# A selective-scan layer followed by linear attention: softplus, the front part and the transfers out moved by a slot, diagonal weights cut into 32x32 blocks

## The chip, the core and the metric

The kernel runs on one core of one Trainium2 chip. The metric is the device time of one launch in microseconds (us). The time before is the median of three runs, 8220.86 us, with runs from 8218.34 to 8221.85 us. PE is TensorE, DVE is VectorE, ACT is ScalarE, POOL is GpSimd, and SP is the engine that issues most of the transfers; "PEq" or "SPq" is the instruction queue of such an engine.

## What is computed

The input x has 4 images, 512 channels and 64 x 64 positions, so 4096 positions in a row. Two residual layers follow each other. Cut to what matters:

```
# layer 0: x = x + L0(group_norm(x))
xn     = layer_norm(tokens)                         # over 512 channels
chunks = 4 groups of 128 channels per image         # 16 sequences of 4096 positions
xi, z  = chunks @ in_proj                           # 256 inner channels each
xc     = silu(causal_conv4(xi))
dt, B, C = split(xc @ x_proj)                       # rank 8, 16 states, 16 states
dt     = softplus(dt @ dt_proj + b)
h[t]   = exp(dt[t] * A) * h[t-1] + dt[t] * xc[t] * B[t]    # 256 channels x 16 states
y[t]   = sum over states of h[t] * C[t]  + xc[t] * D
out    = (y * silu(z)) @ out_proj + skip * chunks
L0     = layer_norm(out) @ proj + b
# layer 1: x = x + L1(group_norm(x))
q, k, v = tokens @ w_qkv + b                        # 8 heads of 64
q, k    = relu(q), relu(k)
kq      = k^T q per head ;  out = (v @ kq) / (sum(kq) + eps) @ w_out + b
```

## The kernel before

The work is cut into 128 steps, `steps = [(b, t, c)]`: image b, tile t of 512 positions (8 per image), channel group c (4). A step has 16 slots (`SLOTS`). For half e of the inner channels (2), for four states at a time (index q, 4), a pair of blocks jj (2) makes one slot g. Partitions hold 32 channels x 4 states, so one slot covers two of the four blocks j of 32 channels.

`slot` (L596) issues, for each slot:

- on POOL, `drive(g + 2)` (L588): the product `bx` of dt*x and B for two blocks; after the second slot of a pair also the copy `st` of the last state and the product of the last 128 columns of `h` with C (L620, L621);
- on DVE, two scans over 512 positions (L610). A scan reads its decay `dA` from PSUM;
- on ACT, after each scan, the decay `dA` of the scan three further on (L584, exp), since there are three `dA` banks;
- on DVE, between the two scans, `product(g - 1)` (L628): `h` times C in the first 384 columns, with C in the PSUM bank `c_all`. After an odd g, it has PE make the next `c_all` (`c_row`, L573; there is one such bank), and then PE adds the states up into `y` (`fold_states`, L639; 4 matmuls side by side).

`AWAY = (2, 10)` names the slots after which DVE may take a long normalization operation. In the slot behind it, `BEHIND = [3, 11]`, the product isn't between the next slot's scans but at the end of the slot itself:

```
if i == 0 and g and (g - 1) % SLOTS not in BEHIND:
    product(g - 1, last)
...
if g % SLOTS in BEHIND:
    product(g, last)
after()
```

Everything else is issued in `after` (L987), at the end of slot s, in program order on each engine's queue: `time_banks` (L486, two PSUM banks `pt`: dt @ dt_proj) in slot 1, `time_steps` (L493, the softplus, between two loads of ACT's function table, L1006 and L1008) in slot 2, `to_rows` (L499, dt and dt*x written to DRAM) and `out_proj` (L661) in slot 3, `with_skip` (L667, the bank `po` read by ACT) in slot 4, and one piece of the `front` (`inputs`, L454: the convolution `pc` in four taps per half, then `pz`) in each of the slots 2, 4, 5, 6, 7 and 8. Slot 10 has `silu` with a table load on each side (L927, L1028), slot 12 and later the pieces of `mixers` (L516). `spread` (L507) loads dt and dt*x back from DRAM, spread over the states, in slot 9 for the next step's first half and in slot 1 for the second.

The other work comes from generators in the queues `ahead`, `late`, `rest` and `light`: the next tile's group and layer norm (`tile_norm`, `normed` L404, `group_norm` L326), the projection after the scan (`projected`, L417), the statistics, and the `attention` of the image before (L682). A piece runs where a credit of matmul work and the count of banks held (`room`, L107, against `limit`) allow. `later(n, what)` (L86) puts an action n slots further on, mostly the eviction of a bank. `po`, `pt`, `pc`, `pz` and all banks of the queues come from one pool of three banks, `ps_w`, taken in turn.

## Time and profile before

| what | value |
|---|---|
| time, median of 3 runs | 8220.86 us (8218.34 to 8221.85) |
| the profiled execution | 8214.62 us |
| its span, first to last instruction | 8212.9 us |
| mean granted TensorE clock | 0.874 |
| DVE busy | 7185.7 us (87%) |
| POOL busy | 6889.7 us (84%) |
| PE busy | 6659.6 us (81%) |
| ACT busy | 5346.7 us (65%) |
| span before the first scan, and after the last | 123 us, 462 us |

The span falls into three parts: 123 us until the first scan, 7627 us of scans, and 462 us after the last scan, in which only the attention of the last image is left. A step takes 59.6 us on average (7627 / 128). The time of the scans' part is the busy time of DVE in it and DVE's idle time; the lines that show this stand in the prediction.

### The profile page before, as it was taken

What the parts mean: (1) busy time and instruction counts of PE and PEld (TensorE: products, weight loads), DVE (VectorE), ACT (ScalarE), POOL (GpSimd) and SP (SyncE); (2) the same over time, 40 slices, a digit from 0 to 9 for tenths busy, and PEclk for the clock granted to TensorE, in tenths of its full rate; (3) what the DMA queues carried; (4) which work ended last, traced back from release to release, by engine and by line L of the source; (5) the groups of instructions that cost most, each with busy time, mean ns of one, the idle gap of its engine ahead of it and who ended that gap; (6) DMA issues with size and microseconds to landing.
All of it is one profiled execution on the core that took longest, in us unless ns stands there. A gap on an engine that the chain in (4) does not pass through costs nothing.

```text
span 8212.9 us, 87683 instructions
## 1 busy us (share of the span) xinstructions
PE 6659.6 (81%) x22496; PEld 2253.4 (27%) x22496; DVE 7185.7 (87%) x6890; ACT 5346.7 (65%) x7841; POOL 6889.7 (84%) x4597
## 2 busy tenths in 40 slices
PE   5677777777888888887788888888788888889699
PEld 1122222112233222332232323332123232333144
DVE  5999999999999999989999999998989999989700
ACT  4666667666676667666677766676766777666421
POOL 4999899999898888889999888888989998888700
PEclk8788878788899989998798999899889998989799
DMA  5666666666666656676666666567666666676412
GB/s 160 161 164 156 151 147 152 155 152 163 158 172 152 156 152 155 171 186 155 168 149 173 162 153 155 151 177 181 153 159 157 156 149 149 153 180 179 116 41 88
DMA packets 829308, 1266.18 MB, mean 154 GB/s; under 512 B 183920, under 2 KB 317568, under 8 KB 816512
## 3 DMA queue, kind: packets, MB, share of 16 engines
q1 hardware_dynamic: 804736, 1222.32, 58.9%
q0 software_dynamic: 16896, 33.56, 2.4%
q10 hardware_dynamic: 7168, 4.71, 0.2%
q8 instruction: 176, 2.88, 0.2%
q14 instruction: 332, 2.72, 0.1%
HBM read 1053.28 MB, written 206.57 MB: 153 GB/s over the span
## 4 chain that ended last, share of the span: by engine, by line
PE 27%; DMA 17%; DVE 17%; POOL 13%; issue 9%; ACT 9%; SPq 8%; POOLq 0%; DVEq 0%; ACTq 0%
DVE h L610 11%; DMA d_all<-d_rows 9%; POOL bx L592 8%; PE pq L120 5%; PE y L120 5%; DVE h L633 5%; SPq L559 5%; PE pc L120 4%; ACT dA L584 4%; DMA b_all<-b_rows 3%; PE pr L120 3%; SPq L513 3%; POOL h L621 2%; PE po L120 2%; PE pp L120 2%
## 5 line engine op out<-in xcount | busy, mean ns | idle before, releaser
L592 POOL TENSOR_TENSOR bx<-d_all,b_all 128x1024 f32<-128x1024 f32 x2048 | 4809.0, 2369 | 92.5 <-DVE h L610 77.1
L610 DVE TENSOR_TENSOR_SCAN h<-dA,st,bx 128x512 f32<-128x512 f32 x3584 | 4436.6, 1271 | 207.2 <-ACT dA L584 191.2
L584 ACT ACTIVATE dA<-d_all,a_t 128x512 f32<-128x512 f32 x4096 | 2765.5, 688 | 1629.8 <-DVE h L610 1579.3
L633 DVE TENSOR_TENSOR h<-h,c_all 128x768 f32<-128x768 f32 x2048 | 1913.9, 935 | 153.2 <-PE c_all L120 142.5
L120 PE MATMUL y<-h,fold 128*32 128x512 f32 x8192 | 1327.3, 725 | 273.2 <-POOL h L621 269.1
L621 POOL TENSOR_TENSOR h<-h,c_sb 128x512 f32<-128x512 f32 x1024 | 1298.4, 1268 | 188.9 <-DMA c_sb<-c_rows 70.6
L120 PE MATMUL c_all<-parts,sel 128*128 128x384 bf16 x1024 | 378.5, 370 | 978.6 <-DVE h L633 977.6
L120 PE MATMUL pc<-xn,w_cv 128*128 128x512 f32 x2048 | 1021.4, 628 | 38.9 <-ACT res L858 12.7
L120 PE MATMUL pq<-w_qk,xa 128*128 128x512 f32 x2048 | 1005.6, 625 | 1.6 <-ACT xa L329 1.6
L610 DVE TENSOR_TENSOR_SCAN h<-dA,bx 128x512 f32<-128x512 f32 x512 | 602.8, 1210 | 76.4 <-ACT dA L584 66.3
L120 PEld LDWEIGHTS <-sel 128*128 128x128 bf16 x1280 | 127.4, 100 | 1710.1 <-DVE h L633 1445.7
L120 PEld LDWEIGHTS pc<-xn,w_cv 128*128 128x128 f32 x2048 | 379.7, 198 | 708.6 <-issue 518.5
L620 POOL COPY st<-h 128x4 f32<-128x4 f32 x1024 | 208.5, 204 | 410.9 <-DVE h L610 383.1
L120 PEld LDWEIGHTS pq<-w_qk,xa 128*128 128x128 f32 x2048 | 404.6, 200 | 476.3 <-issue 449.6
L120 PE MATMUL pr<-xb,m 128*128 128x512 f32 x1024 | 505.0, 633 | 6.2 <-DMA xb<-x 4.2
L120 PE MATMUL pp<-xn,w_pr 128*128 128x512 f32 x1024 | 492.5, 613 | 3.8 <-DVE xn L391 3.8
L120 PE MATMUL pt<-dt,w_dt 32*128 32x512 f32 x512 | 378.2, 943 | 141.2 <-ACT parts L539 126.8
L120 PEld LDWEIGHTS y<-h,fold 128*32 128x32 f32 x8192 | 173.5, 116 | 866.1 <-POOL h L621 446.0
L708 ACT ACTIVATE kq<-pq 128x512 f32<-128x512 f32 x256 | 151.7, 593 | 339.9 <-PE pq L120 338.7
L120 PE MATMUL y<-xz,dg 128*128 128x512 f32 x512 | 364.8, 804 | 0.0
L657 POOL TENSOR_TENSOR xz<-xz 128x512 f32<-128x512 f32 x256 | 325.0, 1270 | 2.7 <-ACT xz L654 2.7
L502 POOL TENSOR_TENSOR dt<-dt,xz 128x1024 f32<-128x1024 f32 x128 | 302.6, 2364 | 25.4 <-DMA c_rows<-dt 20.8
(155 smaller groups left out, 6203.3 us busy)
## 6 DMA issues: line engine op xcount, KB each, us to landing
d_all<-d_rows SPq DMA_DIRECT2D x2048, 256.0 KB, 6.5
b_all<-b_rows SPq DMA_DIRECT2D x4096, 64.0 KB, 2.1
d_rows<-dt SPq DMA_DIRECT2D x256, 512.0 KB, 3.0
c_sb<-c_rows SPq DMA_DIRECT2D x4096, 16.0 KB, 1.8
xs<-in_x_dram SPq DMA_DIRECT2D x32, 1024.0 KB, 7.6
xn<-in_x_dram SPq DMA_DIRECT2D x32, 1024.0 KB, 6.5
xr<-in_x_dram POOLq DMA_DIRECT2D x32, 1024.0 KB, 8.9
x<-xr SPq DMA_DIRECT2D x32, 1024.0 KB, 6.6
```

The lines of the kernel that those rows point to most:

```text
L120: nc.tensor.matmul(out_, lhsT, rhs, **how)
L502: nc.gpsimd.tensor_tensor(f["both"][:, 1], f["both"][:, 0], f["xz"][:, 0], ALU.mult)
L513: nc.sync.dma_start(d[k * BLK : (k + 1) * BLK, v], src)
L559: nc.sync.dma_start(dst[k * BLK : (k + 1) * BLK, :], rows_[q * KS + k, :].partition_broadcast(BLK))
L584: nc.scalar.activation(dAs[k], fs[n]["d_all", e][:, 0, j, :], AF.Exp, scale=a_t[:, e, j, q : q + 1])
L592: nc.gpsimd.tensor_tensor(bxs[g], fs[n]["d_all", e][:, 1, jj * 2 : jj * 2 + 2, :], bc(b_all[g // JJ], 2), ALU.mult)
L610: nc.vector.tensor_tensor_scan(h[:, j, :], dAs.pop(2 * g + i), bxs[g][:, i, :], 0.0 if t == 0 else st[:, c, e, q, j : j + 1], ALU.mult, AL ...
L620: nc.gpsimd.tensor_copy(st[:, c, e, q, :], h[:, :, T - 1])
L621: nc.gpsimd.tensor_tensor(h[:, :, CUT:], h[:, :, CUT:], bc(c_sb.pop(g // JJ), NJ), ALU.mult)
L633: nc.vector.tensor_tensor(own, own, bc(c_all[g // JJ], 2), ALU.mult)
L657: nc.gpsimd.tensor_tensor(f["xz"][:, 1, e, :], f["xz"][:, 1, e, :], f["xz"][:, 0, e, :], ALU.mult)
L708: nc.scalar.activation(qk[i], pq, AF.Relu)
```

## The change

What it does, part by part:

1. The softplus and its two table loads are issued in slot 3 instead of 2, `time_banks` in slot 2 instead of 1, `to_rows` and `out_proj` in slot 4 instead of 3, `with_skip` in slot 6 instead of 4, and the front's pieces in slots 3, 5, 6, 7, 8 and 9. `AWAY` becomes (3, 10), so `BEHIND` becomes [4, 11].
2. `normed` waits two slots between the load of a tile and the first operation on it, `projected` one slot before its accumulating transfer.
3. `to_rows`, `mixers` and `store` issue their transfers to DRAM one slot later than the operation that makes the data; `store` frees its bank before that.
4. The tile `res` has two buffers instead of one.
5. Evictions of attention banks issued in slots 5 to 11 are put two slots later instead of one (`soon`).
6. `limit` is 1 in slots 1 to 5 instead of 15 and 0 to 3, and the pieces marked "two ahead" may start in slot 15 and no longer in 14.
7. The diagonal weights `dg` (D) and `skd` (skip) are kept as 128 x 32 tiles, and each diagonal product is four matmuls of 32 x 32 instead of one of 128 x 128. `ones`, `bqk` and `ident` take less room.

The diff, with a line of context around each edit:

```diff
+    def soon():
+        return 2 if now[0] is not None and 5 <= now[0] % SLOTS < 12 else 1
     def until(*done):
...
     work = {"mm": 0.0}
+    def diagonal(out_, w, rhs):
+        for k in range(P // BLK):
+            r = slice(k * BLK, (k + 1) * BLK)
+            mm(out_[r, :], w[r, :], rhs[r, :], abreast=P // BLK, start=True, stop=False)
...
-    ident = const.tile([P, P], F32, tag="ident", name="ident")
+    ident = wk.tile([P, P], F32, tag="sq", name="ident", bufs=4)
     make_identity(nc, ident)
-    ones = const.tile([P, LANE], F32, tag="ones", name="ones")
+    ones = const.tile([P, 1], F32, tag="ones", name="ones")
     nc.vector.memset(ones, 1.0)
...
     dpar = column(d_par, NH, "dpar")
-    dg = const.tile([P, NH, P], F32, tag="dg", name="dg")
+    dg = const.tile([P, NH, BLK], F32, tag="dg", name="dg")
     for e in range(NH):
-        nc.vector.tensor_scalar(dg[:, e, :], ident, dpar[:, e : e + 1], None, ALU.mult)
+        nc.vector.tensor_scalar(dg[:, e, :], fold, dpar[:, e : e + 1], None, ALU.mult)
     g_sb = column(norm_g, NC, "g_sb")
     b_sb = column(norm_b, NC, "b_sb")
-    skd = ident
+    skd = const.tile([P, BLK], F32, tag="skd", name="skd")
     a_sb = rows(a_log, wk.tile([P, NH, NST], F32, tag="sq", name="a_sb", bufs=4))
...
-    bqk = const.tile([P, 2 * C], BF16, tag="bqk", name="bqk")
-    b_all = wk.tile([P, 2 * C], F32, tag="bx", name="b_all", bufs=3)
-    nc.scalar.dma_start(b_all, b_qkv[0 : 2 * C].partition_broadcast(P))
+    bqk = const.tile([P, C], BF16, tag="bqk", name="bqk")
+    b_qk = wk.tile([P, C], F32, tag="bx", name="b_qk", bufs=3)
+    nc.vector.memset(b_qk, 0.0)
+    for i in range(P // LANE):
+        nc.scalar.dma_start(
+            b_qk[i * LANE : i * LANE + 2, :], b_qkv[0 : 2 * C].rearrange("(j c) -> j c", j=2)
+        )
     bv = column(b_qkv[2 * C : 3 * C], NC, "bv")
...
-    nc.vector.tensor_copy(bqk, b_all)
+    nc.vector.tensor_copy(bqk, b_qk)
     for i in (2, 3):
         r = slice(i * LANE, P)
-        nc.vector.tensor_tensor(b_all[r, :], b_all[r, :], bqk[r, :], ALU.subtract)
-        nc.vector.tensor_copy(bqk[r, :], b_all[r, :])
+        nc.vector.tensor_tensor(b_qk[r, :], b_qk[r, :], bqk[r, :], ALU.subtract)
+        nc.vector.tensor_copy(bqk[r, :], b_qk[r, :])
...
             )
-    nc.vector.tensor_scalar(skd, ident, sk, None, ALU.mult)
+    nc.vector.tensor_scalar(skd, fold, sk, None, ALU.mult)
...
                 mm(
-                    sums[c * LANE : (c + 1) * LANE, :], ones, parts[c],
+                    sums[c * LANE : (c + 1) * LANE, :], ones.to_broadcast([P, LANE]), parts[c],
                     start=True, stop=True, abreast=NC,
...
         nc.sync.dma_start(body, cols(x, b)[:, :, t * T : (t + 1) * T])
+        yield from pause(2)
         yield "free"
...
         yield from until(*taken)
+        yield from pause(1)
...
+        both = f["both"]
         if v:
...
         d_rows = dram.tile([P, NH, T], F32, tag=f"d_rows{v}", name=f"d_rows{v}_{nm}")
-        nc.sync.dma_start(d_rows, f["both"][:, v])
         f["d_rows", v] = d_rows
+        later(1, lambda: nc.sync.dma_start(d_rows, both[:, v]))
...
         b_rows = f["b_rows"] = dram.tile([NST, T], F32, tag="b_rows", name=f"b_rows_{nm}", bufs=3)
-        nc.sync.dma_start(b_rows, dtr[RANK : RANK + NST, :])
         c_rows = f["c_rows"] = dram.tile(
...
         )
-        nc.sync.dma_start(c_rows, dtr[LANE : LANE + NST, CUT:])
+        def rows_out():
+            nc.sync.dma_start(b_rows, dtr[RANK : RANK + NST, :])
+            nc.sync.dma_start(c_rows, dtr[LANE : LANE + NST, CUT:])
+        later(1, rows_out)
         parts = f["parts"] = wk.tile([P, CUT], BF16, tag="parts", name=f"parts_{nm}", bufs=3)
...
     SLOTS = NH * NQ * JJ
-    AWAY = (2, 10)
+    AWAY = (3, 10)
     BEHIND = [s + 1 for s in AWAY]
...
             ys[n, e] = ps_y.tile([P, T], F32, tag="y", name=f"y_{n}_{e}")
-            mm(ys[n, e], dg[:, e, :], fs[n]["xz"][:, 0, e, :], start=True, stop=False)
+            diagonal(ys[n, e], dg[:, e, :], fs[n]["xz"][:, 0, e, :])
         h = hs.pop(g // JJ)
...
         po = f["po"] = work_bank(f"po_{nm}", 0)
-        mm(po, skd, xn[:, c, NTAP - 1 : NTAP - 1 + T], start=True, stop=False)
+        diagonal(po, skd, xn[:, c, NTAP - 1 : NTAP - 1 + T])
         for e in range(NH):
...
                     )
-            return later(1, lambda: add(pk, v == 0))
+            return later(soon(), lambda: add(pk, v == 0))
...
                 pq = work_bank(f"pq_{b}_{i}")
-                mm(
-                    pq, sel[:, 0, 0:1].to_broadcast([P, P]), bqk[:, j * C : (j + 1) * C],
-                    start=True, stop=False,
-                )
+                mm(pq, sel[:, 0, j * BLK : j * BLK + 1].to_broadcast([P, P]), bqk, start=True, stop=False)
                 for c in range(NC):
...
                 qk[i] = both[:, 1 + i % 3, :]
-                ready[i] = later(1, lambda i=i, pq=pq: relu(i, pq))
+                ready[i] = later(soon(), lambda i=i, pq=pq: relu(i, pq))
                 if u:
...
-        kqn = wk.tile([P, NC, P], F32, tag="res", name=f"kqn_{b}", bufs=1)
+        kqn = wk.tile([P, NC, P], F32, tag="res", name=f"kqn_{b}", bufs=2)
         nc.gpsimd.memset(kqn, 0.0)
...
         def store(t, o, pp):
-            res = wk.tile([P, T], F32, tag="res", name=f"res_{b}_{t}_{o}", bufs=1)
+            res = wk.tile([P, T], F32, tag="res", name=f"res_{b}_{t}_{o}", bufs=2)
             nc.scalar.activation(res, pp, AF.Identity, bias=ob[:, o : o + 1])
-            nc.sync.dma_start(cols(out, b)[:, o, t * T : (t + 1) * T], res)
             free()
+            later(1, lambda: nc.sync.dma_start(cols(out, b)[:, o, t * T : (t + 1) * T], res))
...
                         yield "more"
-                later(1, lambda t=t, o=o, pp=pp: store(t, o, pp))
+                later(soon(), lambda t=t, o=o, pp=pp: store(t, o, pp))
                 fetch(t + 1, "b")
...
                             gate(before, 1)
-                        if nxt is not None:
-                            time_banks(nxt, names[n + 1])
                     if s == 2 and nxt is not None:
+                        time_banks(nxt, names[n + 1])
+                    if s == 3 and nxt is not None:
                         nc.scalar.preload_act_table_set("softplus")
...
                         nc.scalar.preload_act_table_set("natural_log_exp_and_others")
-                    if s == 4 and before is not None:
+                    if s == 6 and before is not None:
                         pb_, pt_, pc_ = steps[n - 1]
...
                             add_to(late, leave(pb_, pt_))
-                    if s in (2, 4, 5, 6, 7, 8):
+                    if s in (3, 5, 6, 7, 8, 9):
                         next(front, None)
-                    if s == 3 and nxt is not None:
+                    if s == 4 and nxt is not None:
                         to_rows(nxt, 0, names[n + 1])
                         to_rows(nxt, 1, names[n + 1])
-                    if s == 3 and before is not None:
+                    if s == 4 and before is not None:
                         pb_, pt_, pc_ = steps[n - 1]
...
                         what for k, what in ((0, "wide"), (1, "one ahead"), (2, "two ahead"))
-                        if any(a - 2 * k <= s <= a - k for a in AWAY) or (k == 2 and s >= SLOTS - 2)
+                        if any(a - 2 * k <= s <= a - k for a in AWAY) or (k == 2 and s == SLOTS - 1)
                     ]
...
-                    limit[0] = 1 if s in (SLOTS - 1, 0, 1, 2, 3) else 2
+                    limit[0] = 1 if 0 < s < 6 else 2
                     credit = min(credit + 3.5 - (work["mm"] - seen), 2.6)
```

## Prediction

> **What bounds the kernel now.** I read the page first (part 1, then the costliest groups), then busy time by stretches, DVE's waits in the stretch of the scans, and the timeline where these waits sit.
>
> ```profile
> PE 6659.6 (81%) x22496; PEld 2253.4 (27%) x22496; DVE 7185.7 (87%) x6890; ACT 5346.7 (65%) x7841; POOL 6889.7 (84%) x4597
> ```
>
> The share hides stages, so here is the busy time in the scans up to where attention starts, in the scans after that, and behind the last scan (columns: PE, PEld, DVE, ACT, POOL, clock, DMA share, GB/s):
>
> ```profile
> 123.00:1999.00 1876.00, 1334.47 (x4191) 381.34 (x4191) 1796.09 (x1673) 1279.30 (x1853) 1751.13 (x1168) 0.80 0.64 157
> 1999.00:7750.00 5751.00, 4842.95 (x16680) 1653.58 (x16680) 5322.03 (x5058) 3937.28 (x5795) 5121.44 (x3409) 0.89 0.65 161
> 7750.00:8213.00 463.00, 426.81 (x1508) 195.06 (x1508) 29.26 (x77) 96.92 (x150) 5.08 (x5) 0.95 0.18 59
> ```
>
> DVE is busy 7118 of 7627 us of scans: 93%, POOL 90%. The last 463 us are PE's (92%, at nearly the full clock), the same matmuls before and after. So the change can gain only DVE's idle time in the scans (waits for others, longest first; total, times, longest):
>
> ```profile
> DVE h L610 <- ACT dA L584: 257.5, 146, 49.4
> DVE h L633 <- PE c_all L120: 142.5, 102, 3.7
> DVE kq L715 <- PE pk L120: 78.2, 53, 5.7
> DVE h L610 <- POOL bx L592: 25.1, 25, 2.9
> ```
>
> With small ones it is 544 us. I placed each by counting scans (two a slot, 32 a step):
>
> | DVE waits for | slot | us | waits |
> |---|---|---|---|
> | dA | 3 and 4 | 101 | 44 |
> | dA | 6 | 42 | 31 |
> | dA | 12 | 42 | 42 |
> | c_all | 3 | 30 | 20 |
> | c_all | 7 | 78 | 37 |
> | pk | 5, 6, 10 | 31 | 16 |
> | pk, c_all, dA, bx | 13 to 15 | 102 | 89 |
> | pob, pm, gr | 3 to 5 | 36 | 25 |
> | first decay 49, the rest | | 82 | |
>
> The two costliest, looked at. ACT in a step with c = 0 (idle in brackets):
>
> ```profile
> 1280.34 1.52 ACT L329 ACTIVATE xn<-xn,off_a,gr_a 128x512 f32<-128x512 f32 x2 [2.20 <-DMA xn<-in_x_dram]
> ...
> 1283.06 1.28 ACT L1006 ACT_TABLE_LOAD   x1
> 1284.36 1.26 ACT L495 ACTIVATE dt<-pt,dtb 128x512 f32<-128x512 f32 x2
> 1285.64 1.28 ACT L1008 ACT_TABLE_LOAD   x1
> 1286.94 1.52 ACT L329 ACTIVATE xn<-xn,off_a,gr_a 128x512 f32<-128x512 f32 x2
> ```
>
> and DVE in the same microseconds:
>
> ```profile
> 1289.07 2.46 DVE L610 TENSOR_TENSOR_SCAN h<-dA,st,bx 128x512 f32<-128x512 f32 x2 [3.13 <-ACT dA L584]
> ```
>
> The group norm first waits for its load, then its second half follows the softplus, and the decays come behind both. Of the 44 waits, 39 (98 us) are in the steps with c = 0; softplus alone never made DVE wait, and with one more eviction ahead of it, 0.65 us. Slot 7, on PE and on DVE:
>
> ```profile
> 1181.09 1.88 PE L120 MATMUL pc<-xn,w_cv 128*128 128x512 f32 x4
> 1182.81 1.88 PE L120 MATMUL pp<-xn,w_pr 128*128 128x512 f32 x4
> 1184.52 0.33 PE L120 MATMUL c_all<-parts,sel 128*128 128x384 bf16 x1
> ```
>
> ```profile
> 1184.89 0.95 DVE L633 TENSOR_TENSOR h<-h,c_all 128x768 f32<-128x768 f32 x1 [3.32 <-PE c_all L120]
> ```
>
> c_all stands in PE's queue behind the front and the projection. Starts 1.72 us apart for two full matmuls make a unit of 0.86 us.
>
> **The change, part by part.** DVE's own work stays, so the sum is over its waits. A scan holds DVE 1.19 us and a product 0.85 (distances of their starts). T is the end of slot 3's second scan.
>
> *Group norm behind its load, softplus in slot 3.* Moving with it: two table loads of 1.28, two softplus, and `to_rows` with its POOL product (2.36) and two transfers. The pause takes out the wait for the load (80.5 us of ACT). But in the instruction order of the changed kernel, half of the group norm is still issued behind the softplus, in slot 3, the other half in slot 4. Softplus and loads take 3.88 us; the decay behind them is ready at T + 5.3 and DVE wants it at T + 5.27 plus its extra work there: no slack, as before. With half a group norm (1.43) ahead, DVE waits 1.4 us if it has no statistics (1.2) or long operation (2.18) there. Counted over the steps, 11 are late: **101 becomes 14 us** (0 to 40). The load leaves in slot 0 and is used in slot 3, 10 us later, against 6.5 to land; with that cover gone it costs the old 2.7 us per tile. The two transfers of `to_rows` (512 KB each) now stand in SP's queue behind the b_all and c_sb loads of slots 4 and 5 instead of ahead of them.
>
> *`with_skip` in slot 6, `out_proj` in 4.* ACT waited 105 us for `po`; with a slot more, **42 becomes 10** (0 to 30).
>
> *PE's load.* I counted units between one c_all and the next in both orders (mean over steps, a group of four side by side as one):
>
> | c_all of slot | 0 | 2 | 4 | 6 | 8 | 10 | 12 | 14 |
> |---|---|---|---|---|---|---|---|---|
> | before | 3.5 | 4.9 | 10.6 | 6.0 | 5.0 | 3.6 | 7.4 | 3.7 |
> | after | 3.5 | 6.9 | 7.9 | 6.2 | 5.7 | 3.5 | 7.1 | 3.9 |
>
> The peak of 10.6 (14 in one step of ten) is what slot 7 waits for. At 7.9 units, 6.8 us plus 0.35 for c_all, against 7.65 us of DVE work from slot 4's product to slot 7's, only heavy steps (9 to 10 units) are late: 37 by 0.65 us, 24 in all; at 0.95 a unit (clock 0.9) 50 by 1.3, 64 in all. **78 becomes 35** (15 to 80). Slot 3: **30 becomes 25** (15 to 35).
>
> *A new wait in slot 4.* With `AWAY` 3, slot 4 holds product(3) between its scans and product(4) at its end. Product(3) frees the c_all bank, so product(4) needs a c_all made within one scan; before, slots 2 and 3 shared one, and the next had 3.6 us. Behind this wait on DVE are slot 5's scans, and through them dA, bx and all else. In PE's queue ahead of that c_all stand `pt`, half of `pc` and attention's matmuls. The three banks go round: after two for `pt`, the second further bank taken must wait until the softplus in slot 3 has read the first `pt`, T + 2.8. The trace of before has this wait in small (PE for L495, 44 us with the weight loads). In the changed order, 84 of 127 steps take two or more. With 1, 2 or 4 units behind it, c_all is ready at T + 4.0, 4.9 or 6.6; DVE wants it at T + 3.23 plus its extra work. Steps with a long operation in slot 3 are covered (2.18). Step by step, 37 are late, by 1 to 3.4 us: **0 becomes 89** (30 to 150; the wait overlaps those for dA, of which I counted only the excess).
>
> *Slot 12.* The table loads around silu make DVE wait where it has nothing extra in slot 10: 17 such steps 0.85 us each, and 19 with an eviction `xr` ahead (0.67 us) 1.20 each. The last `pz` copy (0.58) now moves in front of silu in every step, while `soon` takes the `xr` away: 39 x 1.2, **42 becomes 50** (40 to 90; upper end: ACT also waits for `pz`).
>
> *Two-slot evictions, the limit.* pk in 5, 6, 10: **31 becomes 10** (5 to 30). Slots 13 to 15: 12's load falls from 7.4 to 7.1: **102 becomes 90** (50 to 110). Small ones at 3 to 5 and the rest: **118 becomes 100** (85 to 130).
>
> *Transfers later, two `res` buffers.* SP waited 245 us (b_rows), 169 (`res`) and 60 (d_rows) at the head of its queue, holding up the b_all and c_sb loads behind: POOL waited 71 us for c_sb, 55 for `xr` outside the end. DVE waited only 25 us for POOL, so I give this nothing beyond the terms above. Cover: d_rows now leaves 4 slots (13 us) before `spread` reads it, and lands in 3.0 us, 6.6 at most; `b_rows` has a dozen slots. In the end stretch ACT waits 61 us for output transfers, but PE's wait for ACT there is at most the row's 12.7: 0 to 13, taken as 0. Before the first scan: ±5, taken as 0.
>
> *Diagonals.* 384 diagonal products, 256 in `y` and 128 in `po`. `pt` pairs on rows 0 and 32 of the array took 2.08 us for both at half clock where one full product took 1.92: row groups run side by side, but into two banks. `y<-h,fold` has four column groups in one bank, 8 instructions in 1.07 us. Neither is four row groups in one bank. The Trainium skill (page PSUM — Partial Sum Buffer, section "PSUM bank collisions raise a hardware error") quotes that column tiles may share a bank at once, but "different row tiles are not able to access the same PSUM bank at the same time". By the rows the diagonal costs one pass as now, plus a change of array shape: the first instruction of `pt` took 0.69 against 0.59, 0.1 x 384 = 38 us of PE, mostly in slack. By the rule, one after the other, it costs three passes more, 2.6 us. I take the rows, since each block has its own columns and partitions too; the rule is the rival below. No gain on PE either way.
>
> Sum after: 14 + 10 + 25 + 35 + 89 + 50 + 10 + 90 + 100 = 423, from 544: 121 less. The profiled execution, 8214.6, becomes 8094; the median lies 6 above it, so **8100 us** (-1.5%). POOL needs 53.7 us a step (6873 / 128) and the step would take 58.6, so it doesn't take over.
>
> **Rivals.**
> 1. *The wait in slot 4 doesn't come* (c_all early enough as PE's idle shows, or hidden in other waits). For: PE waits 978 us for DVE at c_all rows, so it is often ahead. Against: the bank of `pt`. Then 14 for 89, and slot 7 at 15: 8100 - 95 = 8005.
> 2. *Slot 4 takes it all back*: 150, and 80 in slot 7, since waits on PE meet the half clock (0.80 to 0.89 granted). 8100 + 61 + 45 = 8206, no difference.
> 3. *Slower: diagonals run one after the other.* PE gets 2.6 us more ahead of c_all in slots 4 and 6. In slot 6's stretch 6.8 + 0.35 + 2.6 = 9.7 against 7.65: 2.1 x 126 = 265; in slot 4's some 1.2 x 64 = 80. 8100 + 345 = 8445. It decides from about 1.4 us more per diagonal (0.5 slack, and 121 / 128 to eat the gain). For: the rule. Against: the rows of `pt` and `fold`.
> 4. *The order isn't as meant*: group norm is still behind softplus; that is in the sum.
>
> **How the numbers follow.** Forecast 0.60 (own range 8040 to 8160), rival 1 0.20, rival 2 0.13, rival 3 0.07. The bounds added up one way would reach 7950 and 8310; cut to 8 in 10, 7990 to 8200. What a measurement can tell from no change is 0.2%, 16 us. Faster by more: 0.60 + 0.20 + 0.05 of rival 2; slower: 0.07 + 0.01 of it; 0.07 within.
>
> **What would show it.** Right: DVE waits for dA in slots 3, 4 and 6 together below 50 us; for c_all in slot 7 below half; new waits of L655 for c_all at the end of slot 4, in steps with c = 0 or 3, 2 us each; PE waiting for the softplus row some 40 times or more; ACT's waits for xn's load and for `res` transfers near zero in the scans. Wrong: `y<-xz,dg` rows lasting over 3 us for eight instructions; c_all waits at slot 4 in steps with a long operation; POOL bx waits over 60 us.

## The result, and the profile after

The changed kernel takes 8101.42 us (median of 4 runs, 8097.51 to 8103.36), beside 8219.6 us of the kernel before (8215.61 to 8221.85, 4 runs): ratio 0.9856, 95% interval 0.9839 to 0.9873, 118 us less. The forecast was 8100. The sum under it holds less well than the total, so the profile first. The profiled run took 8103.21 us with a span of 8101.5.

Part 1 of the page, after:

```profile
PE 6487.2 (80%) x24800; PEld 2116.5 (26%) x24800; DVE 7158.1 (88%) x6891; ACT 5365.5 (66%) x7841; POOL 6888.6 (85%) x4597
```

The same three stretches by busy time (PE, PEld, DVE, ACT, POOL, granted clock, DMA share, GB/s); the scans now end at 7631 us:

```profile
119.00:1999.00 1880.00, 1317.96 (x4851) 352.17 (x4851) 1824.07 (x1702) 1307.62 (x1889) 1782.42 (x1190) 0.80 0.66 159
1999.00:7631.00 5632.00, 4682.76 (x18329) 1542.67 (x18328) 5268.42 (x5029) 3927.24 (x5759) 5093.09 (x3390) 0.91 0.66 164
7631.00:8101.00 470.00, 435.23 (x1508) 199.17 (x1508) 28.59 (x76) 97.06 (x150) 4.90 (x5) 0.92 0.18 58
```

The time came out of the scans: 7627.4 us before, 7512.0 after. DVE's waits fell from 544 to 453 us (353 waits to 273; 49 and 46 us of them are the wait of the very first scan, which lies ahead of this part), its busy time (overlap taken off) from 7119 to 7093. The start is 4 us shorter; the end stretch is 8 us longer, at a mean clock of 0.92 instead of 0.95. That is not the change: e5 below leaves that part as it was before, and has 470.9 us at a clock of 0.92 too.

DVE's longest waits in the scans after (total, times, longest; most of the pk row, left out, is the end stretch):

```profile
DVE h L655 <- PE c_all L124: 293.5, 172, 5.7
...
DVE h L632 <- ACT dA L606: 105.4, 54, 46.2
...
DVE h L632 <- POOL bx L614: 12.1, 12, 3.4
```

dA fell by 152 us and c_all rose by 151. Placed by counting scans, as for the forecast (`pk` is attention's bank for k^T q):

| DVE waits for | before | forecast | after |
|---|---|---|---|
| dA, slots 3 and 4 (slot 5 after) | 101 | 14 | 8 |
| dA, slot 6 | 42 | 10 | 0 |
| c_all, slot 3 | 30 | 25 | 0 |
| c_all, end of slot 4 (new) | 0 | 89 | 204 |
| c_all, slot 7 | 78 | 35 | 54 |
| dA, slot 12 | 42 | 50 | 48 |
| pk in 4 to 6 and 10 | 31 | 10 | 6 |
| slots 13 to 15 | 102 | 90 | 46 |
| small ones, first decay, rest | 118 | 100 | 87 |
| sum | 544 | 423 | 453 |

What went, on ACT in a step with c = 0: the group norm no longer waits for its load. It stands behind the softplus with two decays between its halves.

```profile
1265.84 1.26 ACT L512 ACTIVATE dt<-pt,dtb 128x512 f32<-128x512 f32 x2
1267.12 1.28 ACT L1027 ACT_TABLE_LOAD   x1
1268.42 1.52 ACT L344 ACTIVATE xn<-xn,off_a,gr_a 128x512 f32<-128x512 f32 x2
1269.85 1.28 ACT L606 ACTIVATE dA<-d_all,a_t 128x512 f32<-128x512 f32 x2
1271.07 1.50 ACT L344 ACTIVATE xn<-xn,off_a,gr_a 128x512 f32<-128x512 f32 x2
```

What came, at the end of slot 4 of the same step, is product(4) behind a late c_all; the wait is the bracket:

```profile
1269.55 0.95 DVE L655 TENSOR_TENSOR h<-h,c_all 128x768 f32<-128x768 f32 x1 [2.38 <-PE c_all L124]
```

This is the step of the forecast (c = 0 or 3, two units ahead, 2 us each). Over all steps the wait has 67.0 us with c = 0, 50.4 with c = 1, 44.2 with c = 2 and 42.2 with c = 3. The steps with c = 1 and 2 were forecast as covered, because DVE has its long operation in slot 3 there. Here is one, PE and then DVE:

```profile
2233.51 3.78 PE L124 MATMUL pc<-xn,w_cv 128*128 128x512 f32 x4 [2.92 <-DVE xn L406]
2237.23 1.70 PE L124 MATMUL mu_sums_b<-xn,ones 128*32 128x512 f32 x8
2238.86 0.34 PE L124 MATMUL c_all<-parts,sel 128*128 128x384 bf16 x1
```

```profile
2231.20 2.26 DVE L406 TENSOR_TENSOR xn<-xn,var_a 128x2048 f32<-128x2048 f32 x1
...
2239.23 0.95 DVE L655 TENSOR_TENSOR h<-h,c_all 128x768 f32<-128x768 f32 x1 [2.54 <-PE c_all L124]
```

The long operation (L406, the layer norm's multiply by its factor) reads that factor, `var`, from a bank of the pool of three. The softplus banks hold the other two, so `pc` starts only when L406 ends. The long operation delays DVE and, through the bank, PE, so it hides little: the wait is 1.5 us on average over the steps with c = 1 and 2, and 1.7 over those with c = 0 and 3. PE's waits for that row and for the softplus:

```profile
PE pc L124 <- DVE xn L406: 127.2, 61, 3.2
PE pc L124 <- ACT dt L512: 47.0, 27, 2.9
```

### The profile page after: what moved, and what is told of

Its sections match the earlier page's. It is cut to its first block, busy times and chain, and to the rows that moved or that the text cites. A ratio compares the mean times of both kernels' runs of the same rounds, so it can differ in the third digit from the quotient of the medians.

```text
span 8101.5 us, 92105 instructions
## 1 busy us (share of the span) xinstructions
PE 6487.2 (80%) x24800; PEld 2116.5 (26%) x24800; DVE 7158.1 (88%) x6891; ACT 5365.5 (66%) x7841; POOL 6888.6 (85%) x4597
## 4 chain that ended last, share of the span: by engine, by line
DVE 21%; PE 19%; DMA 19%; POOL 15%; issue 10%; SPq 9%; ACT 6%; POOLq 0%; DVEq 0%; ACTq 0%
DVE h L632 13%; POOL bx L614 11%; DMA d_all<-d_rows 11%; DVE h L655 6%; SPq L581 6%; PE pq L124 5%; DMA b_all<-b_rows 4%; SPq L531 3%; ACT dA L606 3%; PE pc L124 3%; PE pr L124 3%; PE y L124 2%; DMA c_sb<-c_rows 2%; POOL h L643 2%; POOL dt L520 1%
## 5 line engine op out<-in xcount | busy, mean ns | idle before, releaser
L632 DVE TENSOR_TENSOR_SCAN h<-dA,st,bx 128x512 f32<-128x512 f32 x3584 | 4425.2, 1268 | 59.0 <-ACT dA L606 49.5
L655 DVE TENSOR_TENSOR h<-h,c_all 128x768 f32<-128x768 f32 x2048 | 1908.8, 932 | 301.9 <-PE c_all L124 293.5
L124 PE MATMUL y<-h,fold 128*32 128x512 f32 x8192 | 1287.8, 705 | 140.7 <-POOL h L643 136.9
L124 PE MATMUL pc<-xn,w_cv 128*128 128x512 f32 x2048 | 1068.2, 657 | 189.4 <-DVE xn L406 127.2
L632 DVE TENSOR_TENSOR_SCAN h<-dA,bx 128x512 f32<-128x512 f32 x512 | 601.6, 1207 | 60.3 <-ACT dA L606 55.9
L124 PE MATMUL y<-xz,dg 32*32 32x512 f32 x2048 | 340.5, 741 | 0.0
L124 PE MATMUL pd<-xz,w_xp 128*128 128x512 f32 x512 | 317.3, 752 | 7.8 <-ACT xz L946 7.8
```

What stands on the lines that cost most here:

```text
L124: nc.tensor.matmul(out_, lhsT, rhs, **how)
L632: nc.vector.tensor_tensor_scan(h[:, j, :], dAs.pop(2 * g + i), bxs[g][:, i, :], 0.0 if t == 0 else st[:, c, e, q, j : j + 1], ALU.mult, AL ...
L655: nc.vector.tensor_tensor(own, own, bc(c_all[g // JJ], 2), ALU.mult)
```

## The experiments

In each, the run of the kernel before on the same chip was 8219 to 8223 us (median). "Waits" are DVE's waits in the scans, by slot as in the table. The figures behind a time are its ratio to the kernel before and the 95% interval of that; the intervals reach some 0.0015 to each side, 12 us, so smaller differences between two runs aren't told apart.

**The diagonals (e4).** The kernel before with the 32x32 blocks alone:

```
-            mm(ys[n, e], dg[:, e, :], fs[n]["xz"][:, 0, e, :], start=True, stop=False)
+            diagonal(ys[n, e], dg[:, e, :], fs[n]["xz"][:, 0, e, :])
-        mm(po, skd, xn[:, c, NTAP - 1 : NTAP - 1 + T], start=True, stop=False)
+        diagonal(po, skd, xn[:, c, NTAP - 1 : NTAP - 1 + T])
```

> The kernel before with one edit alone: the diagonal products of D and of skip as four matmuls of 32x32. Theory A (the four blocks run side by side in one bank): y<-xz,dg busy about 1.4 us per product as now, PE busy within 50 us of 6660, time 8220 within 16 us. Rival D (four row groups of one bank go one after the other): PE busy higher by 384 x 2.6 = 1000 us, time about 8500 us or more.

Measured: 8224.06 us (8217.13 to 8233.55), ratio 1.0009 (1.0 to 1.0018); waits 543 us. The `y` rows of before, of e4, and of the changed kernel:

```profile
L120 PE MATMUL y<-xz,dg 128*128 128x512 f32 x512 | 364.8, 804 | 0.0
```

```profile
L120 PE MATMUL y<-xz,dg 32*32 32x512 f32 x2048 | 370.4, 802 | 0.0
```

```profile
L124 PE MATMUL y<-xz,dg 32*32 32x512 f32 x2048 | 340.5, 741 | 0.0
```

Per diagonal product (256 of them) that is 1.43, 1.45 and 1.33 us. One after the other would have been three passes more, 2.6 us. So the four blocks run side by side, in one PSUM bank. Rival 3 is out, and for this form, in which each block of rows has its own columns and partitions, the measurement decides against the sentence that the prediction quoted from the Trainium skill (page PSUM — Partial Sum Buffer, section "PSUM bank collisions raise a hardware error"). That the blocks would then run one after the other was the prediction's own reading of that sentence, which speaks only of access at the same time. No part of the 118 us comes from here.

**The placement of product(4) (e1, e2).** e1 puts the product back behind slot 3's scans, e2 (`BEHIND = [11]`) puts neither product at the end of its slot:

```
-    BEHIND = [s + 1 for s in AWAY]
+    BEHIND = [3, 11]
```

> The changed kernel with BEHIND = [3, 11] instead of [4, 11]; AWAY stays (3, 10). Product(3) is then at the end of slot 3, so the next c_all is issued to PE ahead of slot 3's front and attention matmuls, and product(4) follows between slot 5's scans. Theory A (the 204 us of waits for c_all at the end of slot 4 come from where the product stands: one scan after the c_all bank came free, and behind slot 3's matmuls in PE's queue): that wait falls below 20 us, slot 7's rises from 54 to about 100 because its stretch on PE gets slot 3's matmuls back, time about 7950 us. Rival B (PE's load and the bank held by softplus set the pace, the place only decides where DVE waits): the 204 us turn up in slots 5 to 7 and the time stays within 20 us of 8101.

> The changed kernel with BEHIND = [11]: product(4) between slot 5's scans, c_all issued where it was. It gets one scan (1.19 us) more. Theory A: each of the 95 waits gets shorter by 1.19 us, 204 us become about 101, slot 7 up by some 15, time about 8010 us. Rival B: the time stays within 20 us of 8101, as the waits move on to slot 7.

Measured: e1 8178.03 us (0.9949, 0.9934 to 0.9964), e2 8086.24 us (0.9836, 0.9821 to 0.9851). In e2 the wait falls from 204 to 116 as theory A has it, but slot 7 rises from 54 to 105 and little is gained: 15 us by the medians, with overlapping intervals. In e1 the wait is gone, but slot 7 has 164 us, slot 9 has 43, dA in slots 5 and 6 has 72 and pk 41: 77 us slower, which neither theory forecast.

**PE's order (e7).** The first half of `pc` moves behind the c_all that product(4) needs:

```
-                    if s in (3, 5, 6, 7, 8, 9):
+                    if s in (4, 5, 6, 7, 8, 9):
                         next(front, None)
```

> The changed kernel with one number changed: the first half of the first convolution (pc) is issued in slot 4 instead of slot 3, so it stands behind the c_all that product(4) needs in TensorE's queue, not ahead of it. Theory A: the wait of product(4) (204 us) is the wait of pc for a bank that the long operation or the softplus still holds: it falls below 60 us in all four kinds of steps; slot 7, with pc's two units more ahead of its c_all, rises from 54 to about 100: 8101 - 95 = about 8005. Theory B: TensorE's load and bank waits in slots 3 to 7 together set the pace: slot 7 takes nearly all (from 54 to 170 or more), and the time is within 20 of 8101.

Measured: 8157.37 us (0.9918, 0.9904 to 0.9932). The wait of product(4) falls from 204 to 45, slot 7 rises from 54 to 203. The row over all places is the same as the changed kernel's 293.5:

```profile
DVE h L655 <- PE c_all L124: 293.1, 169, 5.3
```

Theory B in its mechanism, though the time is 56 us worse, not equal: dA and busy time rose by 27 and 16 us. Moving matmuls about the c_all of slot 4 moves the wait and does not remove it.

**No banks for the queues in slots 2 to 5 (e8).** On top of e2:

```
-                    limit[0] = 1 if 0 < s < 6 else 2
+                    limit[0] = 0 if 1 < s < 6 else 2
```

> The changed kernel with product(4) between the scans of slot 5 (as in e2, 8086 us) and no bank for attention, projection or normalization taken in slots 2 to 5 (limit 0 there instead of 1). Theory A: their matmuls ahead of the c_all of slots 4 and 6 are what is late in slots 5 and 7 (221 us in e2), and later slots have room for them: these waits fall below 80 us and slots 8 to 15 rise by 40 at most: about 8000. Theory B: the work of these queues is needed on time and the slots 6 to 15 are full: the waits move there (slots 8 to 15 rise by 130 us or more), or attention spills behind the last scan and lengthens the end stretch of 470 us: 8090 to 8200.

Measured: 8184.22 us (0.9949, 0.9937 to 0.9962). c_all in slot 5 73 us, slot 7 none, slot 9 136; dA 50 in slot 5 and 69 in slot 12; statistics of `xr` wait 30. The end stretch stays at 470 us. Theory B's shift, with slot 9 as the place.

**The bank that the long operation frees (e9, e10).** The factor goes to SBUF, the order of the instructions is unchanged; e10 adds `BEHIND = [11]`:

```
-            nc.scalar.activation(var, rs, AF.Exp, scale=-0.5)
+            nc.scalar.activation(rs, rs, AF.Exp, scale=-0.5)
-        nc.vector.tensor_tensor(v, v, bc(var, NC), ALU.mult)
+        nc.vector.tensor_tensor(v, v, bc(rs, NC), ALU.mult)
```

> The changed kernel with the result of the exponential (the factor of the layer norm) written to SBUF instead of back into its PSUM bank; the long operation multiplies from there, so the bank that the next convolution (pc) takes comes free one to two slots earlier. The order of the instructions is the same. Theory A (the bank that the long operation frees is what makes product(4) late in the steps with c = 1 and 2): TensorE's waits for L406 (127 us) fall below 15, the waits of product(4) in steps with c = 1 and 2 from 95 to under 35 us, all of them from 204 to about 140, and slot 7 stays near 54: 8101 - 60 = about 8040. Theory B (the load of slots 2 to 7 sets the pace, as e7 showed for another edit): slot 7 takes most of it (54 to 110 or more): within 20 us of 8101. If the long operation costs more from SBUF than the 2.26 us it has now, by 0.3 us or more, that is 128 x 0.3 = 38 us against both.

> e9 together with e2 (product(4) between the scans of slot 5; 8086 us alone). Theory A: the two causes add: 116 + 105 us of waits in slots 5 and 7 fall to about 140 together: 8000 to 8020. Theory B: within 20 us of 8086.

Measured: e9 8107.96 us (0.986, 0.9846 to 0.9873), e10 8075.37 us (0.9822, 0.9808 to 0.9835). In e9's list of PE's longest waits, L406 no longer stands (it was third, with 127 us):

```profile
PE c_all L124 <- DVE h L655: 1193.2, 530, 11.3
PE y L124 <- POOL h L643: 176.1, 200, 3.6
PE pc L124 <- ACT dt L512: 50.0, 26, 2.9
```

The wait of product(4) is 3.8 us in steps with c = 1 and nothing with c = 2 (95 before this edit), still 113 with c = 0 and 3. All of it is 117 (204), and slot 7 stays at 57. The time did not follow, because the long operation got slower, by far more than the 0.3 us that the expectation allowed for (which also multiplied by 128; there are 64). The row of the changed kernel, then that of e9:

```profile
L406 DVE TENSOR_TENSOR xn<-xn,var_a 128x2048 f32<-128x2048 f32 x32 | 72.3, 2260 | 8.3 <-ACT var_a L400 8.3
```

```profile
L406 DVE TENSOR_TENSOR xn<-xn,rs_a 128x2048 f32<-128x2048 f32 x32 | 103.8, 3243 | 6.5 <-ACT rs_a L400 6.5
```

One us more in 64 operations is 64 us, and DVE's busy time is up by 64, while all waits fell by 63.

The slower operation also covers part of the wait, since product(4) itself comes later. In the steps with c = 1 and 2, counted from the end of slot 3's second scan, DVE is ready for product(4) at 5.4 us on average in the changed kernel and at 6.4 in e9; c_all is ready at 6.8 and at 5.8. That c_all comes 1.0 us earlier although everything on DVE is 1.0 us later shows the bank to be the cause. With DVE's times of the changed kernel and c_all's of e9, step by step, 26 of the 95 us would be left; that is an estimate from the two traces, and no run has the early bank without the slow operation.

Why is it slower? In e9's timeline, before the scans, where POOL has no work beside it, the operation takes 2.29 us; beside POOL's `bx` products it takes 3.27:

```profile
69.17 2.29 DVE L406 TENSOR_TENSOR xn<-xn,rs_a 128x2048 f32<-128x2048 f32 x1 [6.54 <-ACT rs_a L400]
```

```profile
2235.33 3.27 DVE L406 TENSOR_TENSOR xn<-xn,rs_a 128x2048 f32<-128x2048 f32 x1
```

```profile
2231.76 4.69 POOL L614 TENSOR_TENSOR bx<-d_all,b_all 128x1024 f32<-128x1024 f32 x2
2236.38 2.26 POOL L642 COPY st<-h 128x4 f32<-128x4 f32 x1
```

POOL's product ends 1.1 us after DVE's operation starts; then POOL's copy of 512 numbers (0.20 us on average in the changed kernel) lasts until the operation ends. All 62 of these operations within the scans show it: each lasts what POOL's product has left when it starts (0.56 to 2.01 us) plus 2.15 us, to 0.01 us. The 58 of POOL's copies that overlap them last 2.25 us on average, the other 966 last 0.20. So one holds up the other in turn, whole instructions at a time. That such a pair contends, for an exclusive lock, is what the Trainium skill (page SBUF — State Buffer, section "Who interferes with whom") states for a VectorE instruction with two SBUF inputs beside a GpSimd instruction that reads SBUF.

e10, where the c_all waits of slots 5 and 7 are 72 and 73 (116 and 105 in e2), is 11 us faster than e2 by the medians (the two intervals overlap) and 26 us faster than the changed kernel, with an interval just below that one's. Theory A's sum (8000 to 8020) did not come: the two waits fell to 145 us as it has it, but the slower operation took most of that back.

**The group norm's pause alone (e5).** The kernel before, with the group norm two slots behind its load:

```
         nc.sync.dma_start(body, cols(x, b)[:, :, t * T : (t + 1) * T])
+        yield from pause(2)
         yield "free"
...
-            assert c != 2 or not ahead
+            assert c != 3 or not ahead
```

The second edit lets the next tile's pieces reach into the step with c = 2; e3, the pause without it, gave no result.

> The kernel before with one edit: the group norm of the next tile is issued two slots behind its load (the softplus stays in slot 2, nothing else moves). Theory A: the waits for dA in slots 3 and 4 of the steps with c = 0 (98 us of before) come from the group norm standing in ACT's queue with its load still under way, and DVE gets them back wherever they stood: 98 to under 20, time 8219 - 80 = about 8140. Theory B: TensorE's load ahead of c_all in slots 5 to 7 sets the pace of these slots, so the wait turns up again as one for c_all in slot 7 (78 us in before becomes 130 or more): 8190 to 8220.

Measured: 8209.68 us (0.9983, 0.9977 to 0.999), waits 538. The waits for dA in slots 3 to 5 fell from 103 to 24 us, in the steps with c = 0 from 98 to 10, as theory A has it. The gain did not come, though not by way of slot 7's c_all, which fell to 53. Now the layer norm's mean is late for the long operation on it (48 of these 54 us are in the scans), the waits for bx rose from 25 to 50, and those for c_all in slots 3 and 15 from 56 to 96:

```profile
DVE xn L371 <- PE mu_a L120: 54.4, 19, 6.4
```

Alone, the pause is worth 13 us. In the changed kernel no wait for `mu_a` is among the scans' waits; which of the other moves takes it away was not tried.

**The transfers and the buffers (e6, e11, e12).** e6 is the changed kernel with all moves in the slots undone. It keeps the transfers out one slot later, the two output buffers and the diagonals (and the smaller constants and the slot's pause ahead of `projected`'s accumulating load, which its expectation did not name):

```
-        yield from pause(2)
-    AWAY = (3, 10)
+    AWAY = (2, 10)
-                    if s == 3 and nxt is not None:
+                    if s == 2 and nxt is not None:
                         nc.scalar.preload_act_table_set("softplus")
...
```

> The changed kernel with all of its moves in the slots undone (front, softplus, products for the rows, out_proj, with_skip, AWAY, limit, two-slot evictions and the pause back as before); what stays are the transfers out one slot later, the two output buffers and the 32x32 diagonals. Theory A (the forecast): these give nothing beyond the moves: 8205 to 8225, DVE waits in the scans as before (544 us) within 25. Theory B: DVE's busy time, 26 us less in the changed kernel, and part of its waits come from transfers that no longer block SP's queue: 8150 to 8190, with DVE busy near 7093 us in the scans.

e11 undoes the late transfers in the changed kernel, e12 the second buffer (`kqn`, which shares it, follows):

```
-        later(1, lambda: nc.sync.dma_start(d_rows, both[:, v]))
+        nc.sync.dma_start(d_rows, both[:, v])
-        later(1, rows_out)
+        rows_out()
...
-            later(1, lambda: nc.sync.dma_start(cols(out, b)[:, o, t * T : (t + 1) * T], res))
+            nc.sync.dma_start(cols(out, b)[:, o, t * T : (t + 1) * T], res)
```

```
-            res = wk.tile([P, T], F32, tag="res", name=f"res_{b}_{t}_{o}", bufs=2)
+            res = wk.tile([P, T], F32, tag="res", name=f"res_{b}_{t}_{o}", bufs=1)
```

> The changed kernel with its transfers out (d_rows, b_rows and c_rows, out) issued at once, as before; two output buffers stay. Theory A (the forecast): nothing, 8101 within 15; SP's waits at the head of its queue return (some 200 us) but DVE does not see them. Theory B (e6 was 41 us faster than before with only transfers, buffers and diagonals changed): their delay is worth most of it here too: 8120 to 8140, with POOL's waits for c_sb, b_all and xr up by 60 us or more and DVE's for bx and dA up by 20 or more.

> The changed kernel with one output buffer (res) instead of two; the transfers stay one slot later, so ACT has to wait for a whole transfer more often than before. Theory A (the forecast): ACT's waits for res return (105 us or more) but do not reach DVE: 8101 within 15. Theory B: evictions are issued ahead of the decays on ACT, so these waits reach DVE as dA waits of 30 us or more (longer than before the change, since the transfer now starts a slot later): 8130 to 8170.

Measured: e6 8181.15 us (0.995, 0.9936 to 0.9963), e11 8151.01 us (0.9915, 0.9901 to 0.9928), e12 8156.11 us (0.9918, 0.9904 to 0.9931). All three times are on theory B's side: these parts are worth 41 us without the moves, and with the moves 50 us for the transfers and 55 for the buffer (in e12 with the transfers still late; no run undoes both). DVE's busy time in e6, 7111 us, is not theory B's 7093. In e11 POOL's wait for the loads of `c_sb` (C for POOL's part of the product), which stand behind the blocked transfers in SP's queue, is 138 us, against 50 in the changed kernel:

```profile
POOL h L643 <- DMA c_sb<-c_rows: 138.2, 78, 6.1
```

```profile
POOL h L643 <- DMA c_sb<-c_rows: 49.7, 30, 5.3
```

DVE's waits for bx rose from 12 to 37 us, c_all from 294 to 312. In e12 ACT waits for output transfers (77 us of this row in the scans), and behind ACT PE's `pc` waits:

```profile
ACT res L877 <- DMA out_dram<-res: 138.2, 38, 9.3
...
PE pc L124 <- ACT res L877: 60.1, 7, 9.9
```

It is the bank again. With the softplus holding two of the three banks, `pc` needs the one that an output eviction has yet to read, and that eviction waits for its buffer's transfer. One of the seven places, on ACT, PE and DVE:

```profile
3384.85 0.69 ACT L877 ACTIVATE res<-pr,ob 128x512 f32<-128x512 f32 x1 [8.84 <-DMA out_dram<-res]
```

```profile
3385.59 3.78 PE L124 MATMUL pc<-xn,w_cv 128*128 128x512 f32 x4 [9.37 <-ACT res L877]
```

```profile
3391.89 0.95 DVE L655 TENSOR_TENSOR h<-h,c_all 128x768 f32<-128x768 f32 x1 [13.39 <-PE c_all L124]
```

In these seven steps the wait of product(4) is 88 us, against 19 in the changed kernel: nearly all of its rise from 204 to 277. The dA waits (103 us) did not move, so theory B's route was wrong though its size was not.

**Softplus back in slot 2 (e13).** On top of e10:

```
-                    if s == 2 and nxt is not None:
+                    if s == 1 and nxt is not None:
                         time_banks(nxt, names[n + 1])
-                    if s == 3 and nxt is not None:
+                    if s == 2 and nxt is not None:
                         nc.scalar.preload_act_table_set("softplus")
```

> e10 (the factor of the layer norm in SBUF, product(4) between the scans of slot 5; 8075 us) with the time steps one slot earlier again: pt's matmuls in slot 1, softplus in slot 2, as before the change; group norm, front, row products and all else stay. Theory A (softplus itself never made DVE wait in before; in slot 3 it makes pc wait for pt's bank, 50 us on TensorE): with the group norm out of its way it is better early: TensorE's waits for L512 fall from 100 to under 30 us, the waits for c_all in slots 5 and 7 from 145 to about 110, no dA waits in slots 3 and 4: 8035 to 8055. Theory B (the move of softplus is needed: pt in slot 1 waits for pd's bank, which ACT's last copy to parts frees in slot 1, and the decays of slot 4 stand behind the table loads): dA waits of 20 us or more in slots 3 and 4 and TensorE's wait for parts of 100 us or more return: 8070 to 8110.

Measured: 8116.68 us (0.9871, 0.9854 to 0.9887), 41 us slower than e10. Neither theory's reason holds: no dA waits came back in slots 3 and 4 (6 us), and PE waits only 37 us for parts. Slot 5's c_all wait fell from 72 to 12 as in theory A, but slot 3's rose from 1 to 52 and pk's from 6 to 27. With `pt` in slot 1, its load is ahead of the c_all of slot 2. That points to PE's order, and not ACT's, as what the place of softplus is worth; the two were not moved apart.

DVE's c_all waits in slots 3 to 9, and all its waits, over the kernels (us):

| slot | after | e1 | e2 | e7 | e8 | e9 | e10 | e13 |
|---|---|---|---|---|---|---|---|---|
| 3 | 0 | 0 | 2 | 1 | 4 | 2 | 1 | 52 |
| end of 4, 5 | 204 | 0 | 116 | 45 | 73 | 117 | 72 | 12 |
| 7 | 54 | 164 | 105 | 203 | 0 | 57 | 73 | 73 |
| 9 | 4 | 43 | 4 | 22 | 136 | 2 | 6 | 11 |
| sum of these | 262 | 207 | 227 | 271 | 213 | 178 | 152 | 148 |
| all waits | 453 | 513 | 436 | 480 | 539 | 390 | 359 | 401 |

In the changed kernel's order the sum stays between 207 and 271 wherever the wait is; with the bank freed early it is 148 to 178 (in part by the slower operation's cover). It is no fixed sum of the three banks, though: in the kernel before it is 116, and in e6, with the moves undone, 124. There dA and slots 13 to 15 have the waits.

## Why the prediction was right, and where it wasn't

The total came out (8101 against 8100; the own range was 8040 to 8160), by way of several errors that cancel; that it is right to 1 us is luck. The waits fell by 91 us, not 121 (3 of the 91 lie ahead of the scans). With 26 us of DVE's busy time, 4 us at the start and 8 lost at the end the profiled executions are 111 us apart; the medians are 118 apart, since the profiled one of before lies 5 us below its median and that of after 2 above. By e6 the moves themselves are worth 80 us (8181 to 8101) where the sum has 121, and the parts costed at nothing are worth 41.

- *Group norm behind its load, softplus in slot 3: right.* 14 forecast, 8 measured; ACT's wait for the load, 80.5 us before, is gone. e5 shows the same term alone (103 to 24) and that it is worth only 13 us without the moves around it; e13 shows that softplus's place counts, as it seems through PE's order.
- *`with_skip` a slot later: right*, 42 to 0 (10 forecast).
- *The new wait in slot 4: right in kind, place and size per step, wrong in where it comes.* 89 forecast, 204 measured. The steps with c = 0 and 3 have 109 in 42 waits, near the 89 in 37. The step that failed is "Steps with a long operation in slot 3 are covered (2.18)": the bank that PE needs is the one this operation frees, so it delays both. That is the 95 us of the steps with c = 1 and 2, in 53 waits, which the forecast had itself named as a sign of being wrong. e9, where the bank comes free earlier, takes it to 4, about a quarter of that by its slower operation (by the estimate above). The forecast had named only the softplus as the reader to wait for (40 waits; there were 27, and 61 for L406).
- *Slot 7: too low.* 35 forecast, 54 measured, inside its bounds; the sign "below half" (of 78) was missed. e7 shows why the two terms should not have been estimated apart: less in slot 4 is more in slot 7.
- *Slot 3, slots 13 to 15, pk and the small ones: too high* by 25, 44, 4 and 13 us. In slot 3 the count of units, 3.5 ahead of its c_all in both orders, missed a wait of PE: before, `pt` stood ahead of that c_all, and PE waited 127 us in all for ACT's `parts` there, none after; with `pt` back in slot 1, e13 has 37 us of it and 52 us of c_all waits in slot 3. For slots 13 to 15, the two candidates, the limit and the two-slot evictions, were not tried singly. e6 has about 120 us there, so it is the moves and not the transfers.
- *"I give this nothing beyond the terms above" for transfers and buffers: wrong.* Undone, they cost 50 and 55 us. The premise, DVE waits only 25 us for POOL, was right for the kernel before, but the routes are others: a queue that is blocked delays c_sb, `y` and with it c_all, and an ACT that waits for a buffer delays the eviction of the bank that PE needs (e12).
- *Diagonals: right.* No gain, one pass (e4).
- *Busy time, taken as unchanged: off by 26 us.* Scans and products last 0.3% less each (18 us, the rows of L632 and L655 summed), the rest is small operations. The cause is not settled; e6 has 7 us of it, e7 10.

So rival 1 (the wait doesn't come) and rival 2 (slot 4 takes it all back) were both wrong. Slot 4 and slot 7 took 204 + 54, more than rival 2's 150 + 80, and the time still fell because all other terms together came to 195 us where the forecast had 299. Rival 2's reason, waits that meet the half clock, is not in the trace: over DVE's waits for c_all in the kernel before, the granted clock was 0.91 on average, over all the scans 0.87. And the terms' bounds, added up one way, give 7917 and 8372, not the 7950 and 8310 of the text; the forecast does not rest on them.

## What to carry to other kernels

Before a long operation is counted as cover for a late producer, look at what the operation holds: if it frees the buffer that the producer needs, it delays both, and little is covered. Waits for one shared resource in neighbouring slots are best forecast as one sum: in these runs, moving a piece of work within the changed kernel moved the wait (e1, e2, e7, e8), and the sum fell clearly only where the resource was freed earlier (e9, e10). A part whose own wait looks harmless is not worth nothing: the second output buffer, costed at nothing because DVE hardly waited for POOL, is worth 55 us in the changed kernel, since the eviction that waits for it holds a bank.

## What the runs showed of the hardware

- Four 32x32 blocks on the diagonal, each with its own rows, columns and partitions, ran side by side into one PSUM bank: 1.33 us for four in the changed kernel and 1.45 in e4, against 1.43 for one 128x128 product of the same length in the kernel before.
- A VectorE multiply of 128x2048 took 2.26 us with its second operand in PSUM. From SBUF it took 2.29 where GpSimd was idle, and during the scans 2.15 us plus what was left of GpSimd's running product: 3.26 as a median, 2.70 to 4.15 (e9). A GpSimd copy that met it took 2.25 us instead of 0.20. In this kernel the PSUM bank that it holds is paid for with up to 95 us of waits, and the SBUF copy with 64 us of DVE.
- The end stretch, the same matmuls in every kernel, took 469 to 472 us in 13 profiled runs and 462 in that of the kernel before; the granted clock there was 0.95 in the kernel before and 0.92 to 0.93 in the 13.
